# A transformer layer on one core: the turn of the attention output from TensorE to VectorE, two variances from VectorE to ScalarE, and a new order of the work

## The chip, the core and the metric

The kernel runs on one core of one Trainium2 chip. The time is that of the device in microseconds, from one launch of the program. The core has four engines that compute, each with its own queue of instructions in a fixed order: TensorE (PE in the profile, its weight loads PEld), VectorE (DVE), ScalarE (ACT) and GpSimd (POOL). A fifth, SyncE (SP), issues transfers. An instruction that needs another engine's result waits on a semaphore, and all that stands behind it in its queue waits as well.

## What is computed

The input `x` holds 16 sequences of 256 tokens with 256 features. Three residual blocks follow one another, each behind a layer norm:

```python
x = x + attn(layernorm(x))        # a second layer norm with weights inside, 16 heads of 16,
                                  # rotary angles, t = 1 + s + s*s/2 in place of exp, t / sum(t)
x = x + cross(layernorm(x), ctx)  # dec[token] + enc[key] + bias: a sum of two projections to one number
x = x + moe(layernorm(x))         # shared expert + 2 of 16 experts of width 128 for each token
```

In the attention the weighted sum of values `wv` is divided by the sum of the weights of its head and then multiplied by `w_o`. The square in the weights is completed: a = (1 + s/4)^2, and the output adds the sum of the values to each, so that the numerator and (from a column of ones, number 16 of 32) the denominator of every head come out of the same product. All is fp32.

## The kernel before

**Stages.** The first stage is a software pipeline over the 16 sequences. The class `Sequence` has a method for each step, and the list `ORDER` names steps with a lag: (3, "output") in pass i works on sequence i-3. The loop runs over passes i = 0 to 21 (the largest lag is 6) and over the 65 entries of `ORDER` in each; steps whose sequence does not exist are skipped. The schedule is manual: every engine gets its instructions in exactly this order. The list `DRAIN` puts the pieces of the shared expert (`gate_up`, `hidden`, `down`, `add`, for six of eight groups of 512 tokens) between the entries of the last passes, at (pass minus 16, entry). The second stage runs the routed experts by blocks of 128 tokens (`block_tp`, `block_gu`, `block_th`, `block_eo`), which read rows that the first stage wrote to the buffer `listed` in memory (`enlist`), and at the end adds the results. The blocks can begin when the last sequence has been given its places (`place`) and its rows are enlisted.

**A sequence's way**, with lines of the profile. `stat` (L377, L378: two batch-norm operations for each of two token tiles), `scale` (POOL, L384, L385), `norm` (POOL, L393: `h`), `turn_h` (four PE transposes), `copy_h` (ACT, L543), `project` and `project_v` (PE, L553, L601), `sum_values`, `rope` (VectorE, L563 and L569, both read PSUM), `rope_sum` (POOL, L575: `qkr`), `turn_q` and `turn_k` (PE), `copy_q` (L585), `copy_k` (ACT). Then for four groups of four heads `score` (PE, L649), two `square` (ACT, L659) and `product` (PE, L669).

**The steps that the change replaces.** `copy_x` (ACT, L680) brings a pair of groups from PSUM to `xs`, with 32 rows for each head: 16 values, the denominator in row 16, the rest unused. `turn_x` turns a token tile of `xs` with four PE transposes into `xt_ps` (L694). `normalise` takes the reciprocal of column 16 of each head and multiplies (VectorE, L705, L706), from PSUM into `wv`. `turn_w` turns `wv` back with four PE transposes (`tp_w`), and `copy_w` copies it (ACT, L716) to `wvT`, which `output` (PE, L722) multiplies with `wo`. `add_y` (L728) adds to `x`; `decode` computes the statistics of `x` and a weighted sum (L736), `scale_dec` (POOL) scales it, `add_cross` (L748) adds it with `enc_row` and computes the statistics of the third norm; `norm3` (POOL) writes `h3`.

**Routing.** `logits` and `sigmoid` give 16 scores a token; `choose` (VectorE, L792 to L825) finds the two best and marks them in two tiles `hot`; `count` (PE, L784) counts how many tokens ahead chose each expert; `place` (L841 to L881) turns that into row numbers `slots`; `enlist` (POOL, L888) writes rows of `h3` to them, two transfers for each of the two choices.

**Buffers.** PSUM has three one-bank buffers of tag "t", taken in turn by `tp_q`, `tp_k`, `ps_vsum`, `xt_ps`, `pv`, `tp_w`, `ahead`, `pq`, `py`, `tp_h`, `pl`; a step that takes one waits until the third step before it has been read out. Scores have two buffers of two banks, the products one bank.

Of the kernel before, what the change touches and what calls it, by code (L numbers as in the profile page):

```python
# [44 lines left out]
F32 = mybir.dt.float32  # L45
I32 = mybir.dt.int32
AF = mybir.ActivationFunctionType
# [4 lines left out]
P = 128  # L52
# [23 lines left out]
def decoder_kernel(  # L76
# [69 lines left out]

    wo_sb = const.tile([P, KT, D], F32, name="wo_sb")
    for k in range(KT):
        half = w_o[ts(k, P)].rearrange("(j two d) f -> two j d f", two=2, d=HD)
        for i in range(2):  # L150
            nc.sync.dma_start(out=wo_sb[ts(i, P // 2), k], in_=half[i])
# [24 lines left out]
    ones = const.tile([P, P], F32, name="ones")  # L176
# [187 lines left out]
    with tc.tile_pool(name="work", bufs=2) as work, tc.tile_pool(  # L364
# [16 lines left out]
        def rsqrt_eps(var):  # L381

            r = small.tile([P, TT], F32, tag="rs", name="rs")
            nc.gpsimd.tensor_scalar(r, var, 1.0, EPS, ALU.mult, ALU.add)  # L384
            nc.gpsimd.tensor_tensor(r, r, neg_half, ALU.pow)  # L385
            return r

        def normed(h, src, mv, r):

            neg = small.tile([P, TT], F32, tag="neg", name="neg")  # L390
            nc.gpsimd.tensor_scalar(neg, mv[:, :, 0], -1.0, 1.0, ALU.mult, ALU.mult)
            for t in range(TT):
                nc.gpsimd.tensor_scalar(  # L393
                    h[:, t, 0:D], src[:, t], neg[:, t : t + 1], r[:, t : t + 1], ALU.add, ALU.mult
                )
# [72 lines left out]
        class Sequence:  # L468
# [36 lines left out]
            def norm(self):  # L505
                self.h = work.tile([P, TT, D], F32, tag="h", name="h")
                normed(self.h, self.x, self.mv, self.r2)
# [181 lines left out]
            def turn_x(self, q):  # L689
                if q == 0:  # L690
                    self.xt = []
                xt = p_t.tile([P, HEADS, VW], F32, tag="t", name="xt_ps")
                for g in range(GRP):
                    nc.tensor.transpose(  # L694
                        xt[:, ts(g, 4)].rearrange("p h d -> p (h d)"),
                        self.xs[:, g, ts(q, P)], ident,
                    )
                self.xt.append(xt)

            def normalise(self, q):  # L700
                if q == 0:
                    self.wv = work.tile([P, TT, HEADS, HD], F32, tag="wv", name="wv", bufs=1)
                xt = self.xt[q]
                rec = small.tile([P, HEADS], F32, tag="rec", name="rec")
                nc.vector.reciprocal(rec, xt[:, :, HD])  # L705
                nc.vector.tensor_tensor(  # L706
                    self.wv[:, q], xt[:, :, 0:HD],
                    rec.unsqueeze(2).to_broadcast([P, HEADS, HD]), ALU.mult,
                )

            def turn_w(self):
                self.tp_w = self.turned(self.wv.rearrange("p t h d -> p t (h d)"), "tp_w")

            def copy_w(self):
                self.wvT = work.tile([P, KT, T], F32, tag="hT", name="wvT")
                nc.scalar.copy(self.wvT, self.tp_w)  # L716
# [10 lines left out]
            def add_y(self):  # L727
                nc.vector.tensor_tensor(self.x, self.py, self.x, ALU.add)  # L728

            def decode(self):  # L730

                mv = self.mv1 = stats(self.x)
                self.dec = small.tile([P, TT], F32, tag="dec", name="dec")
                for t in range(TT):
                    junk = work.tile([P, D], F32, tag="junk", name="junk_d", bufs=1)
                    nc.vector.scalar_tensor_tensor(  # L736
                        junk, self.x[:, t], mv[:, t, 0:1], mlp_bc[:, D : 2 * D],
                        ALU.subtract, ALU.mult, accum_out=self.dec[:, t : t + 1],
                    )

            def scale_dec(self):
                r = rsqrt_eps(self.mv1[:, :, 1])
# [3 lines left out]
            def add_cross(self):  # L746
                for t in range(TT):
                    nc.vector.scalar_tensor_tensor(  # L748
                        self.x[:, t], self.x[:, t], self.dec[:, t : t + 1], self.enc_row,
                        ALU.add, ALU.add,  # L750
                    )
                self.mv3 = stats(self.x)

            def norm3(self):
                self.h3 = work.tile([P, TT, ROW], F32, tag="h3", name="h3", bufs=3)
                normed(self.h3, self.x, self.mv3, rsqrt_eps(self.mv3[:, :, 1]))
# [23 lines left out]
            def count(self):  # L780

                self.ahead = p_t.tile([P, 2, TT, E], F32, tag="t", name="ahead")
                for i, lhsT in enumerate((tri, ones)):
# [5 lines left out]
            def choose(self):  # L789
# [7 lines left out]
                self.hots = []  # L797
                for i in range(2):
                    hot = tiny_p.tile([P, TT, E], F32, tag=f"hot_{i}", name="hot")
# [13 lines left out]
                    self.hots.append(hot)  # L813
                self.both = tiny_p.tile([P, TT, E], F32, tag="both", name="both")
                nc.vector.tensor_tensor(self.both, self.hots[0], self.hots[1], ALU.add)
# [14 lines left out]
            def place(self):  # L830
# [42 lines left out]
                for i, hot in enumerate(self.hots):  # L873
                    nc.vector.tensor_tensor(hot, hot, rows, ALU.mult)
                    with nc.allow_low_precision(reason="whole numbers below 2**24"):
                        nc.vector.tensor_reduce(self.slots[:, i], hot, AX.X, ALU.add)
# [61 lines left out]
        gate_sb = work.tile([P, D], F32, tag="wv", name="gate_sb", bufs=1)[:E]  # L938
        nc.sync.dma_start(out=gate_sb, in_=gate_w)

        def turn_gate():
# [8 lines left out]
            (2, "rope_sum", 1), (5, "logits"), (1, "copy_h"), (3, "copy_x", 0), (3, "score", 3),  # L950
            (6, "enlist", 0), (1, "project", 0), (2, "turn_q"), (5, "sigmoid"),
            (3, "square", 3, 1), (2, "turn_k"), (0, "load"), (3, "product", 2), (4, "decode"),
            (3, "square", 3, 0), (0, "experts", 0), (2, "copy_q"), (0, "stat"), (1, "encode"),
            (2, "copy_k", 0), (4, "scale_dec"), (3, "product", 3), (2, "copy_k", 1),
            (1, "rope", 0), (3, "copy_x", 1), (1, "sum_values"), (0, "scale"), (2, "score", 0),
            (1, "copy_vsum"), (3, "turn_x", 0), (2, "square", 0, 0), (3, "turn_x", 1),
            (5, "choose"), (6, "enlist", 1), (2, "square", 0, 1), (1, "project_v"),
            (3, "normalise", 0), (0, "norm"), (3, "normalise", 1), (2, "score", 1), (3, "turn_w"),
            (5, "count"), (4, "add_cross"), (5, "place"), (1, "copy_v"), (1, "project", 1),
            (2, "square", 1, 0), (2, "product", 0), (0, "experts", 1), (2, "square", 1, 1),  # L960
            (1, "rope_sum", 0), (3, "copy_w"), (2, "score", 2), (4, "norm3"), (3, "output"),
            (1, "rope", 1), (1, "turn_vsum"), (4, "turn_h3"), (3, "get_enc"), (2, "square", 2, 0),
            (0, "turn_h"), (2, "square", 2, 1), (2, "product", 1), (3, "add_y"), (4, "copy_h3"),
# [4 lines left out]
            (2, 54, 0, "gate_up"), (2, 61, 0, "hidden"), (3, 4, 5, "gate_up"),  # L968
            (3, 14, 1, "gate_up"), (3, 37, 5, "hidden"), (3, 51, 5, "down", 0),
            (3, 51, 1, "hidden"), (3, 54, 4, "gate_up"), (3, 57, 5, "add", 0),  # L970
            (4, 3, 0, "down", 0), (4, 4, 2, "gate_up"), (4, 25, 4, "hidden"), (4, 35, 0, "add", 0),
            (4, 42, 4, "down", 0), (4, 49, 0, "down", 1), (4, 57, 3, "gate_up"),
            (4, 57, 5, "down", 1), (5, 7, 2, "hidden"), (5, 11, 0, "add", 1), (5, 19, 4, "add", 0),
# [267 lines left out]
```

## Time and profile before

| | |
|---|---|
| median of 3 runs | 517.9 us (517.79 to 518.06) |
| the profiled execution | 515.8 us, its span from first to last instruction 514.0 us |
| TensorE clock granted | 0.997 |
| busy PE / PEld / DVE / ACT / POOL | 487.7 / 340.8 / 391.0 / 305.7 / 305.2 us |
| first `qT` copy (L585), then in passes 6 and 7 | 23.73, 96.43, 116.13 us |
| end of the last `place` / first `block_gu` | 363.04 / 375.73 us |

All times inside the run are from the start of the span. A row such as "L636 DVE STREAM_TRANSPOSE vsum<-vsum_rows 128x128 ... x16 | 4.8, 302 | 0.0" is a group of instructions: line, engine, operation, written<-read, shape, number; then busy us in all and mean ns of one; then the engine's idle time ahead of them and what ended it. A row in order of time has its start and length in us first, and in brackets the idle time before it. Rows of one engine may overlap a little, because the next instruction starts while the last drains; so costs on a full engine are taken from start to start.

### The profile page before, as it was taken

What the parts mean: (1) busy time and instruction counts of PE and PEld (TensorE: products, weight loads), DVE (VectorE), ACT (ScalarE), POOL (GpSimd) and SP (SyncE); (2) the same over time, 40 slices, a digit from 0 to 9 for tenths busy, and PEclk for the clock granted to TensorE, in tenths of its full rate; (3) what the DMA queues carried; (4) which work ended last, traced back from release to release, by engine and by line L of the source; (5) the groups of instructions that cost most, each with busy time, mean ns of one, the idle gap of its engine ahead of it and who ended that gap; (6) DMA issues with size and microseconds to landing.
All of it is one profiled execution on the core that took longest, in us unless ns stands there. A gap on an engine that the chain in (4) does not pass through costs nothing. (4 is left out here: it accounts for less than half of the span.)

```text
span 514.0 us, 13014 instructions
## 1 busy us (share of the span) xinstructions
PE 487.7 (95%) x4270; PEld 340.8 (66%) x4270; DVE 391.0 (76%) x1703; ACT 305.7 (59%) x639; POOL 305.2 (59%) x491
## 2 busy tenths in 40 slices
PE   2899999999999999999999999898889999999995
PEld 1456666666766666666666666554578888888883
DVE  5723659988988888988988898899865557777767
ACT  2376776776866767767667767511245555555540
POOL 5743554777768668668668636554326666556560
PEclk9999999999999999999999999999999999999998
DMA  5877255234234233233111011111275457768865
GB/s 177 276 247 223 86 167 164 67 115 135 65 105 134 66 114 116 85 104 104 44 53 55 28 29 54 49 47 43 77 204 171 137 166 268 257 244 281 263 201 201
DMA packets 61138, 69.68 MB, mean 136 GB/s; under 512 B 7164, under 2 KB 52493, under 8 KB 61072
## 3 DMA queue, kind: packets, MB, share of 16 engines
q1 hardware_dynamic: 53760, 50.88, 32.0%
q0 software_dynamic: 6624, 17.05, 9.1%
q10 hardware_dynamic: 688, 0.92, 0.5%
q8 instruction: 35, 0.57, 0.5%
q14 instruction: 31, 0.25, 0.2%
HBM read 36.89 MB, written 33.24 MB: 136 GB/s over the span
## 5 line engine op out<-in xcount | busy, mean ns | idle before, releaser
L659 ACT ACTIVATE a<-sc 128x1024 f32<-128x1024 f32 x128 | 124.1, 1022 | 54.3 <-PE sc L649 54.3
L342 POOL DMA_INDIRECT given<-block_got,block_dest x74 | 72.3, 977 | 61.1 <-ACT block_rowsT L290 41.7
L888 POOL DMA_INDIRECT listed<-h,slots x64 | 66.7, 1043 | 28.8 <-issue 24.1
L649 PE MATMUL sc<-qT,kT 32*128 32x256 f32 x1024 | 74.7, 400 | 0.5 <-ACT a L659 0.2
L312 PE MATMUL block_gu<-wgu_sb,block_rowsT 128*128 x288 | 74.3, 381 | 0.0
L575 POOL TENSOR_TENSOR qkr<-rot,m 128x512 f32<-128x512 f32 x32 | 40.6, 1270 | 47.6 <-DVE m L569 47.6
L669 PE MATMUL av<-a,vaug 128*32 128x256 f32 x1024 | 65.6, 384 | 1.2 <-ACT a L659 1.1
L553 PE MATMUL pq<-wqkv,hT 128*128 128x512 f32 x128 | 64.7, 629 | 1.5 <-ACT hT L543 1.5
L649 PEld LDWEIGHTS sc<-qT,kT 32*128 32x128 f32 x1024 | 47.1, 184 | 17.9 <-issue 11.1
L312 PEld LDWEIGHTS block_gu<-wgu_sb,block_rowsT 128*128 128x128 f32 x288 | 49.2, 190 | 4.2 <-ACT block_hid L318 0.2
L331 DVE COPY block_hidT<-block_th 128x128 f32<-128x128 f32 x74 | 21.6, 292 | 39.1 <-PE block_th L329 38.9
L385 POOL TENSOR_TENSOR rs<-rs,neg_half 128x2 f32<-128x2 f32 x64 | 47.6, 744 | 5.3
L669 PEld LDWEIGHTS av<-a,vaug 128*32 128x32 f32 x1024 | 28.1, 109 | 32.5 <-issue 16.6
L335 PE MATMUL block_eo<-wd_sb,block_hidT 128*128 x148 | 44.0, 380 | 0.0
L377 DVE BATCH_NORM_STATS2 st<-x_all 128x6 f32<-128x256 f32 x96 | 39.3, 409 | 3.2 <-DMA x_all<-in_x_dram 2.7
L318 ACT ACTIVATE block_hid<-block_gu 128x128 f32<-128x128 f32 x74 | 20.5, 278 | 35.1 <-PE block_gu L312 32.5
L341 ACT COPY block_got<-block_eo 128x256 f32<-128x256 f32 x74 | 27.6, 373 | 19.2 <-PE block_eo L335 19.1
L393 POOL TENSOR_SCALAR h<-x_all,neg,rs 128x256 f32<-128x256 f32 x64 | 36.6, 575 | 3.3
L553 PEld LDWEIGHTS pq<-wqkv,hT 128*128 128x128 f32 x128 | 22.3, 194 | 23.0 <-issue 15.4
L563 DVE TENSOR_TENSOR rot<-pq,cosf 128x512 f32<-128x512 f32 x32 | 22.0, 687 | 20.1 <-PE pq L553 18.9
L384 POOL TENSOR_SCALAR rs<-mv 128x2 f32<-128x2 f32 x48 | 10.5, 219 | 40.7 <-DVE mv L378 26.1
L680 ACT ACTIVATE xs<-av,vsum 128x256 f32<-128x256 f32 x64 | 27.0, 478 | 9.6 <-PE av L669 9.6
(187 smaller groups left out, 991.9 us busy)
## 6 DMA issues: line engine op xcount, KB each, us to landing
listed<-empty SPq DMA_DIRECT2D x9, 1056.0 KB
block_rows<-listed SPq DMA_DIRECT2D x68, 132.0 KB
sum<-given SPq DMA_DIRECT2D x15, 512.0 KB
x_all<-in_x_dram SPq DMA_DIRECT2D x16, 256.0 KB
c<-in_ctx_dram SPq DMA_DIRECT2D x16, 256.0 KB
out_dram<-x_all SPq DMA_DIRECT2D x15, 256.0 KB
enc_row<-enc_rows SPq DMA_DIRECT2D x16, 128.0 KB
wgu_sb<-in_L_ffn_w_gate_dram SPq DMA_DIRECT2D x16, 128.0 KB
```

Source lines behind the costliest of these rows:

```text
L312: nc.tensor.matmul(gu, lhsT=self.rowsT[:, k], rhs=wgu_sb[:, ds(e, 1), k].rearrange("p a i m -> p (a i m)"), start=(k == 0), stop=(k == KT ...
L335: nc.tensor.matmul(eo, lhsT=self.hidT, rhs=wd_sb[:, ds(self.e, 1)].rearrange("m a d -> m (a d)"), start=True, stop=True,)
L342: ins = nc.gpsimd.indirect_dma_start(out=given, out_offset=bass.IndirectOffsetOnAxis(ap=self.dest, axis=0), in_=got, in_offset=None, bound ...
L377: nc.vector.bn_stats(st, src[:, t])
L385: nc.gpsimd.tensor_tensor(r, r, neg_half, ALU.pow)
L393: nc.gpsimd.tensor_scalar(h[:, t, 0:D], src[:, t], neg[:, t : t + 1], r[:, t : t + 1], ALU.add, ALU.mult)
L553: nc.tensor.matmul(pq.rearrange("p h i two -> p (h i two)"), lhsT=self.hT[:, k, ts(t, P)], rhs=wqkv[:, k, 0 : 2 * D], start=(k == 0), stop ...
L575: nc.gpsimd.tensor_tensor(self.qkr[:, t], self.rot[t].rearrange("p h d -> p (h d)"), self.m2[t].rearrange("p h i two -> p (h i two)"), ALU ...
L649: nc.tensor.matmul(scs[j // 2][:, j % 2, kt], lhsT=self.kT[rows, g % 2, g // 2, ts(kt, P)], rhs=self.qT[rows, g // 2], start=True, stop=True,)
L659: nc.scalar.activation(a, self.scs[g][i], AF.Square, bias=1.0, scale=HD**-0.5)
L669: nc.tensor.matmul(self.av[ts(j, 32), g % 2], lhsT=self.va[:, kt, head], rhs=self.a[g, j // 2][:, j % 2, kt], start=(kt == 0), stop=(kt == ...
L888: ins = nc.gpsimd.indirect_dma_start(out=listed, out_offset=bass.IndirectOffsetOnAxis(ap=self.slots[:, i, t : t + 1], axis=0), in_=self.h3 ...
```

## The change

1. `turn_x`, `turn_w` and `copy_w` are gone. `normalise(half)` works on a pair of groups in SBUF: VectorE transposes `xs` in 32x32 blocks (a token's head then lies in a row of 32), takes the reciprocal, multiplies, and transposes back in blocks straight into `wvT`. In the new layout the rows of `wvT` are in the order of `w_o`, which is loaded in one transfer in place of four.
2. `add_y` and `add_cross` also give the sum over the features of each token. A new step `spread1` or `spread3` on ScalarE takes the mean from it and sums the squares of x minus mean; the batch-norm operations of these two norms are gone. The first norm keeps them.
3. In `place` the two tiles `hot` are one, and their rows are computed in one product and one reduction.
4. `ORDER` is new and has 63 entries; the largest lag is 7, so there is one pass more. `output` and `add_y` go from lag 3 to 4, `add_cross`, `norm3`, `turn_h3` from 4 to 5, `choose`, `count`, `place` from 5 to 6. `logits` and `sigmoid` stay at lag 5 but stand at the end of the pass. `DRAIN` is new.
5. The tile of ones has 16 columns (its first is broadcast in `count`), and `gate_sb` shares the buffer of `xs`.

```diff
+            def normalise(self, half):
+                if half == 0:
+                    self.wvT = work.tile([P, KT, T], F32, tag="hT", name="wvT")
+                n = T // 32
+                xt = work.tile([P, 2, n, 32], F32, tag="xt", name="xt", bufs=1)
+                nc.vector.transpose(
+                    xt.rearrange("p i n f -> p (i n f)"),
+                    self.xs[:, ts(half, 2)].rearrange("p i t -> p (i t)"),
+                )
+                rec = small.tile([P, 2, n], F32, tag="rec", name="rec", bufs=1)
+                nc.vector.reciprocal(rec, xt[:, :, :, HD])
                 nc.vector.tensor_tensor(
+                    xt[:, :, :, 0:HD], xt[:, :, :, 0:HD],
+                    rec.unsqueeze(3).to_broadcast([P, 2, n, HD]), ALU.mult,
+                )
+                nc.vector.transpose(
+                    self.wvT[:, half].rearrange("p (n i f) -> p n i f", i=2, f=HD),
+                    xt[:, :, :, 0:HD].rearrange("p i n f -> p n i f"),
+                )
...
             def add_y(self):
-                nc.vector.tensor_tensor(self.x, self.py, self.x, ALU.add)
+                self.sum1 = small.tile([P, TT], F32, tag="sum1", name="sum1", bufs=2)
+                for t in range(TT):
+                    nc.vector.scalar_tensor_tensor(
+                        self.x[:, t], self.py[:, t], 0.0, self.x[:, t], ALU.add, ALU.add,
+                        accum_out=self.sum1[:, t : t + 1],
+                    )
+
+            def spread(self, name, total, room):
+                neg = small.tile([P, TT], F32, tag=f"neg{name}", name=f"neg{name}", bufs=2)
+                var = small.tile([P, TT], F32, tag=f"var{name}", name=f"var{name}", bufs=2)
+                nc.scalar.activation(neg, total, AF.Copy, scale=-1.0 / D)
+                for t in range(TT):
+                    nc.scalar.activation(
+                        room[:, t, 0:D], self.x[:, t], AF.Square, bias=neg[:, t : t + 1], scale=1.0,
+                        accum_out=var[:, t : t + 1],
+                    )
+                return neg, var
+
+            def spread1(self):
+                self.neg1, self.var1 = self.spread("1", self.sum1, self.wvT)
...
-                for i, hot in enumerate(self.hots):
-                    nc.vector.tensor_tensor(hot, hot, rows, ALU.mult)
-                    with nc.allow_low_precision(reason="whole numbers below 2**24"):
-                        nc.vector.tensor_reduce(self.slots[:, i], hot, AX.X, ALU.add)
+                nc.vector.tensor_tensor(
+                    self.hots, self.hots, rows.unsqueeze(1).to_broadcast([P, 2, TT, E]), ALU.mult
+                )
+                with nc.allow_low_precision(reason="whole numbers below 2**24"):
+                    nc.vector.tensor_reduce(self.slots, self.hots, AX.X, ALU.add)
...
         ORDER = [
+            (0, "load"), (0, "stat"), (5, "add_cross"), (3, "product", 1), (3, "square", 2, 0),
+            (2, "turn_q"), (2, "turn_k"), (2, "copy_q"), (3, "copy_x", 0), (1, "encode"),
+            (4, "output"), (2, "copy_k", 0), (0, "scale"), (6, "choose"), (3, "score", 3),
+            (0, "experts", 0), (2, "copy_k", 1), (3, "square", 3, 0), (4, "add_y"),
+            (3, "square", 3, 1), (0, "norm"), (1, "project", 0), (3, "product", 2), (1, "rope", 0),
+            (6, "count"), (5, "spread3"), (5, "norm3"), (2, "score", 0), (4, "spread1"),
+            (2, "square", 0, 1), (1, "project", 1), (3, "product", 3), (6, "place"),
+            (2, "square", 0, 0), (1, "rope", 1), (3, "copy_x", 1), (1, "sum_values"),
+            (4, "get_enc"), (2, "score", 1), (4, "decode"), (3, "normalise", 0), (1, "project_v"),
+            (7, "enlist", 1), (1, "rope_sum", 0), (1, "copy_vsum"), (2, "square", 1, 1),
+            (0, "experts", 1), (2, "square", 1, 0), (4, "scale_dec"), (0, "turn_h"),
+            (5, "turn_h3"), (3, "normalise", 1), (1, "rope_sum", 1), (1, "copy_v"),
+            (1, "turn_vsum"), (0, "copy_h"), (6, "enlist", 0), (5, "copy_h3"), (2, "product", 0),
+            (2, "score", 2), (2, "square", 2, 1), (5, "logits"), (5, "sigmoid"),
         ]
         DRAIN = [
+            (2, 32, 4, "gate_up"), (2, 56, 4, "hidden"), (2, 61, 5, "gate_up"),
+            (3, 4, 5, "hidden"), (3, 18, 2, "gate_up"), (3, 25, 3, "gate_up"),
+            (3, 40, 4, "down", 0), (3, 40, 3, "hidden"), (3, 50, 4, "add", 0),
+            (3, 57, 4, "down", 1), (4, 13, 4, "add", 1), (4, 16, 3, "down", 0),
+            (4, 23, 3, "add", 0), (4, 39, 2, "hidden"), (4, 56, 5, "down", 0),
+            (5, 19, 5, "add", 0), (5, 21, 1, "gate_up"), (5, 33, 1, "hidden"),
...
```

The order before had, among the entries around these: (3, "turn_x", 0), (3, "turn_x", 1), (3, "normalise", 0), (3, "normalise", 1), (3, "turn_w"), (4, "add_cross"), (5, "place"), (2, "product", 1) near the end, (3, "copy_w"), (3, "output"), (3, "get_enc") and (3, "add_y") last but one.

## The prediction

> **What bounds the kernel now.** I read the page's busy shares and slices first, then the busy time by 20 us windows, then one period in order of time.
>
> ```profile
> PE 487.7 (95%) x4270; PEld 340.8 (66%) x4270; DVE 391.0 (76%) x1703; ACT 305.7 (59%) x639; POOL 305.2 (59%) x491
> ...
> PE   2899999999999999999999999898889999999995
> ...
> DVE  5723659988988888988988898899865557777767
> ```
> ```profile
> 180.00:200.00 20.00, 20.00 (x219) 13.44 (x218) 17.36 (x75) 14.41 (x26) 14.50 (x26) 1.00 0.32 101
> ...
> 320.00:340.00 20.00, 17.25 (x162) 10.75 (x160) 17.38 (x82) 8.30 (x15) 11.30 (x17) 1.00 0.13 47
> ```
> In 180:200 (columns PE, PEld, DVE, ACT, POOL, then clock) PE is never idle, at the full clock, and VectorE is close behind at 17.36. In 320:340 PE has holes and VectorE has not: the tail belongs to VectorE. A third stage, the expert blocks, begins with the first `block_gu` at 375.73 and is PE back to back; the change does not touch it. So what counts is when the last sequence's `place` ends, 363.04 in the timeline.
>
> One period, PE in order of time, then VectorE's groups of operations:
>
> ```profile
> 178.75 1.09 PE L694 MATMUL xt_ps<-ident,xs 128*128 128x128 f32 x8
> 179.68 1.89 PE L601 MATMUL pv<-wqkv,hT 128*128 128x256 f32 x8
> 181.50 1.15 PE L649 MATMUL sc<-qT,kT 32*128 32x256 f32 x16
> 182.58 0.66 PE L533 MATMUL tp_w<-ident,wv 128*128 128x128 f32 x4
> 183.07 0.31 PE L784 MATMUL ahead<-both,tri 128*128 128x32 f32 x2
> ```
> ```profile
> L377 DVE BATCH_NORM_STATS2 st<-x_all 128x6 f32<-128x256 f32 x96 | 39.3, 409 | 3.2 <-DMA x_all<-in_x_dram 2.7
> ...
> L378 DVE BATCH_NORM_AGGREGATE mv<-st 128x2 f32<-128x6 f32 x96 | 17.5, 182 | 3.3
> ...
> L636 DVE STREAM_TRANSPOSE vsum<-vsum_rows 128x128 f32<-128x128 f32 x16 | 4.8, 302 | 0.0
> ...
> L792 DVE STREAM_TRANSPOSE s<-sT 128x64 f32<-128x64 f32 x16 | 3.8, 236 | 0.0
> ```
> The copy `qT` starts at 175.25 and 194.96: the period is 19.71. Start to start, the eight `xt_ps` transposes hold PE for 179.68-178.75 = 0.93 and the four `tp_w` for 0.49.
>
> **PE.** Both go: 1.42 a sequence, so PE's floor falls to 18.29.
>
> **VectorE**, by start-to-start times of the same period. Now: normalise 1.29, add_cross 0.79 and its statistics 1.10, place 4.16, both ropes 2.40, vsum 0.34, add_y 0.73, statistics 1.08, decode 0.91, stat 1.09, encode 1.11, choose 3.40: 18.40, with 1.2 idle.
> - Out: two statistics, -2.18; normalise, -1.29.
> - In, for each of two halves: a 128x512 block transpose, a reciprocal, a product, a 128x256 transpose. No row has these transposes. 64 more columns cost 302-236 = 66 ns, so 512 columns cost 302+6x66 = 0.70 and 256 cost 0.43. Four and two times the 302 row (1.21, 0.60) are the upper ends; the flatter step from the 32-column row (211 to 236) gives 0.60 and 0.40, the lower. I take the slope of the nearest rows. Reciprocal 0.26 and product 0.42 as L705 and L706 have them. With 0.03 between dependent operations: 1.93 a half, 3.86 in all.
> - add_y becomes two additions with sums; decode's pair of the same form takes 0.91, so +0.20. Sums in add_cross: two accumulator reads of 83 ns, 0.12 after overlap.
> - Both choices at once: four operations of 0.19 (0.65 start to start) become two of about 0.22: -0.2.
>
> Sum 18.40-2.18-1.29+3.86+0.20+0.12-0.20 = 18.9. Some of it is not work but blocking: L868, L869, L870, both L810 and L825 have means 0.58 above their neighbours of the same shape. Free of blocking VectorE needs about 18.4, PE 18.3: VectorE becomes the bound, and the blocking decides the period T.
>
> The blocking, in order of time, VectorE then POOL:
>
> ```profile
> 295.49 1.99 DVE L810 TENSOR_TENSOR hot<-hot,h 128x32 f32<-128x32 f32 x1
> ```
> ```profile
> 295.16 0.97 POOL L888 DMA_INDIRECT listed<-h,slots  x1 [0.30 <-DVE hot L805]
> 296.14 1.28 POOL L575 TENSOR_TENSOR qkr<-rot,m 128x512 f32<-128x512 f32 x1
> ```
> A 0.19 us operation with two SBUF inputs lasted until POOL's addition was over (297.42). [...]
>
> In the new order POOL's `h` stands beside choose, the third norm beside rope and place, one `qkr` addition beside the end of place, the other beside the second normalise. The two products move from PSUM to SBUF and can be blocked now. I take 0.7 a period; the ends are 0.1 (all beside rope, transposes and statistics, which show no such lengthening) and 2.0 (both additions met almost in full, 2x1.28, less what VectorE does meanwhile). T = 19.1, from 18.5 to 20.4.
>
> **ScalarE and POOL.** Each variance adds a copy of 0.2 and two squares with sums; L543 has 0.54 for a square-sized operation with sum, so 1.3 twice, less `copy_w` 0.59: +2.0 on 14.1, 16.1 of 19.1. The square waits for add_y; queued behind it are the squares of score group 0, which PE's next product needs only some 3 us later. POOL loses one 0.2 operation. Without this slack each 0.1 would go on T.
>
> **Walk through the new order** with these durations: `project 1` needs add_y's PSUM buffer, `turn_h` rope's, `output` the second normalise of the pass before. All are met if PE runs up to 1.2 ahead of VectorE, so I count no further wait in the period. `get_enc` is issued 28 tasks (some 8 us) ahead of its reader, before 49 tasks; L748 shows no idle time.
>
> **Fill.** Startup to the first `qT` copy (23.73) stays. From there to the fifth copy (96.43) PE worked 72.7 us. Of that 3x1.42 = 4.3 goes, and one output 1.83, one score 1.08, one `tp_h3` 0.5, logits 0.34 and count 0.35 (4.1) move behind the mark, as these steps come a pass later: 64.3, so VectorE's first full pass starts near 87.
>
> **Steady and tail.** Passes 6 to 15 take 10T, pass 16 T-1.1. Then VectorE alone: passes 17 and 18 (add_cross, choose, add_y, place, decode, normalise) 13.5 each, 19 without normalise 9.65, 20 without add_y and decode 7.8, 21 choose and place 6.9; blocking 1.0; four `hidden` (1.4) and four `add` (0.65) of the shared expert ahead of the last place, 8.2; waits 2.4, as before (0.98+0.38+1.00). The last place ends at 87+11T-1.1+51.4+1.0+8.2+2.4 = 148.9+11T. The same addition on the kernel before, from 309.9, gives 364.0 against 363.04.
>
> T = 19.1 gives 359.0: 4.0 earlier. The gains (fill 8, period 11x0.6) are mostly returned by the seventh pass of the pipeline. Behind the last place four enlists (1.28 each) and the first block loads follow as now, 12.7 to `block_gu`; PE's rest in that time (one gate_up 3.6, eight downs of 0.92: 11.0) fits under it. If it did not, the excess would be added. One load of `wo` for four, the smaller `ones` and `gate_sb` in another buffer cost nothing: their readers come tens of us after the loads, and the gate is turned (34.8) before the first `xs` is written.
>
> Span 514.0-4.0 = 510.0, profiled execution 515.8-4.0 = 511.8. The median of the runs lies 2.1 above the profiled time, so 513.9.
>
> **Rivals.**
> 1. Slower: one `qkr` addition meets decode or a product of normalise in full, each pass. Then T = 18.4+0.58+1.0 = 20.0, the last place 368.9, the time 523.8. It decides from T = 19.5, blocking of 1.1. For it: L810 above, and more two-input SBUF work than before. Against: in 180:200 POOL is free a quarter of the time, and blocked orders shift until they meet less. 0.25.
> 2. VectorE slips past POOL, PE is the bound: T = 18.5, last place 352.4, time 507.3. For it: sums of 18.4 and 18.3. 0.20.
> 3. The transposes cost in proportion to size: +2x(0.51+0.17) = 1.36, T = 20.5, +11.4, time 529. The slope of three rows speaks against it. 0.07.
> 4. The longer tail waits 3 to 5 more, since two gate_ups stand ahead of PE's short steps: no change, 518. 0.08.
> The forecast has 0.40.
>
> **Numbers.** Faster 0.40+0.20 = 0.60, same 0.08, slower 0.32; 0.2% is 1 us, about what can be told apart. 506 takes in rival 2, 525 rival 1; rival 3 is left out.
>
> **What would show it.** Right: `qT` copies 18.5 to 19.5 apart, 128x512 transposes near 0.70, VectorE without idle time from pass 6, last place near 359. Wrong: PE idle behind VectorE by over 1 us a period, products of 1 us or more, VectorE idle in the tail by over 5 us, or `block_gu` over 14 us behind the last place.

## The result: 2.9% slower, and where the time went

The changed kernel takes 533.29 us in the median (529.06 to 534.44, four runs) beside 517.85 for the kernel before on the same chip: a ratio of 1.0286, with an interval of 1.0229 to 1.0343. The forecast was 513.9 in a range of 506 to 525. The profiled execution took 533.32, its span is 531.5, 17.5 more than before.

The page after: busy time of the engines, and the rows of TensorE, VectorE and the granted clock in 40 slices of 13.3 us.

```profile
PE 481.8 (91%) x4078; PEld 319.2 (60%) x4078; DVE 417.8 (79%) x1687; ACT 332.9 (63%) x783; POOL 300.6 (57%) x475
...
PE   2899999999899899989998998986889999999994
...
DVE  5736559899999999999999998898745557777766
...
PEclk9999999999999999999999998998979999999999
```

The two engines have changed places: VectorE now stands at 9 from the ninth slice to the twenty-fourth, and TensorE has holes there. The same windows as before, and the one in which the blocks begin:

```profile
180.00:200.00 20.00, 18.17 (x204) 11.22 (x192) 18.66 (x68) 14.96 (x34) 13.56 (x24) 1.00 0.29 88
320.00:340.00 20.00, 18.53 (x180) 9.75 (x173) 16.77 (x82) 14.54 (x34) 10.75 (x17) 0.91 0.10 34
380.00:400.00 20.00, 15.72 (x67) 11.59 (x66) 9.06 (x40) 6.37 (x18) 3.53 (x4) 0.83 0.56 164
```

In 180:200 TensorE is busy for 18.17 of 20, and it waits for VectorE twice a period (here the bracket names the engine that ended the wait):

```profile
185.02 1.06 PE L529 MATMUL tp_h<-ident,h 128*128 128x128 f32 x8 [1.11 <-DVE m L565]
196.98 0.38 PE L796 MATMUL ahead<-both,tri 128*128 128x32 f32 x2 [0.72 <-DVE norm L828]
```

The copies of `qT` start at 127.60 and, eight periods later, at 294.64: the period is 20.88 in place of 19.71. The 17.5 us divide as follows. The last `place` ends at 375.92 in place of 363.04, +12.9. From there to the first `block_gu` (390.01) it is 14.1 in place of 12.7, +1.4. From there to the end 141.5 in place of 138.3, +3.2. The pipeline is the main part, and in it the period; the fill did become shorter (fifth `qT` copy at 89.25, before at 96.43).

Two operations of VectorE carry the period. VectorE first, then GpSimd, in order of time:

```profile
186.75 1.31 DVE L698 TENSOR_TENSOR xt<-xt,rec 128x256 f32<-128x256 f32 x1
...
189.75 0.42 DVE L698 TENSOR_TENSOR xt<-xt,rec 128x256 f32<-128x256 f32 x1
...
200.91 1.83 DVE L876 SCALAR_TENSOR_TENSOR jump<-firsts,ends 128x16 f32<-128x16 f32 x1
```
```profile
186.51 1.27 POOL L571 TENSOR_TENSOR qkr<-rot,m 128x512 f32<-128x512 f32 x1
...
200.44 0.97 POOL L900 DMA_INDIRECT listed<-h,slots  x1 [0.30 <-DVE ends_new L866]
201.43 1.28 POOL L571 TENSOR_TENSOR qkr<-rot,m 128x512 f32<-128x512 f32 x1
```

An operation of `place` on 16 columns, 0.18 long in the tail, takes 1.83 and is over when GpSimd's first `qkr` addition is over (202.71). The first half's product takes 1.31 and the second half's 0.42: the first ends 0.28 behind the end of the second addition (187.78). From here on, *lengthening* is the sum, over VectorE's operations in one period, of what each takes above the shortest operation of its line and shape in the run, counted from 0.06 up. In the period 169.34 to 190.22 it is 2.94: 1.67 in `place`, 0.88 in the product, 0.39 in three small ones. Without it the period would be 17.9.

### The profile page after: what moved, and what is told of

Its sections match the earlier page's. It is cut to its first block, busy times and chain, and to the rows that moved or that the text cites. A ratio compares the mean times of both kernels' runs of the same rounds, so it can differ in the third digit from the quotient of the medians.

```text
span 531.5 us, 12752 instructions
## 1 busy us (share of the span) xinstructions
PE 481.8 (91%) x4078; PEld 319.2 (60%) x4078; DVE 417.8 (79%) x1687; ACT 332.9 (63%) x783; POOL 300.6 (57%) x475
## 5 line engine op out<-in xcount | busy, mean ns | idle before, releaser
L655 ACT ACTIVATE a<-sc 128x1024 f32<-128x1024 f32 x128 | 125.4, 1020 | 36.6 <-PE sc L645 35.7
L665 PE MATMUL av<-a,vaug 128*32 128x256 f32 x1024 | 69.7, 388 | 0.0
L549 PE MATMUL pq<-wqkv,hT 128*128 128x512 f32 x128 | 66.0, 641 | 0.7 <-ACT hT L539 0.7
L645 PEld LDWEIGHTS sc<-qT,kT 32*128 32x128 f32 x1024 | 47.2, 185 | 19.8 <-issue 6.6
L337 ACT COPY block_got<-block_eo 128x256 f32<-128x256 f32 x74 | 27.6, 373 | 19.2 <-PE block_eo L331 19.1
L529 PE MATMUL tp_h<-ident,h 128*128 128x128 f32 x128 | 19.5, 290 | 20.2 <-DVE m L565 10.7
L387 POOL TENSOR_SCALAR h<-x_all,neg,rs 128x256 f32<-128x256 f32 x64 | 35.5, 560 | 3.3
L711 PE MATMUL py<-wo_sb,wvT 128*128 128x256 f32 x128 | 32.0, 390 | 0.8 <-ACT sT L790 0.5
L597 PE MATMUL pv<-wqkv,hT 128*128 128x256 f32 x128 | 31.9, 392 | 0.3 <-ACT vsum_rows L627 0.3
```

The costliest lines, as they stand in the source:

```text
L387: nc.gpsimd.tensor_scalar(h[:, t, 0:D], src[:, t], neg[:, t : t + 1], r[:, t : t + 1], ALU.add, ALU.mult)
L549: nc.tensor.matmul(pq.rearrange("p h i two -> p (h i two)"), lhsT=self.hT[:, k, ts(t, P)], rhs=wqkv[:, k, 0 : 2 * D], start=(k == 0), stop ...
L645: nc.tensor.matmul(scs[j // 2][:, j % 2, kt], lhsT=self.kT[rows, g % 2, g // 2, ts(kt, P)], rhs=self.qT[rows, g // 2], start=True, stop=True,)
L655: nc.scalar.activation(a, self.scs[g][i], AF.Square, bias=1.0, scale=HD**-0.5)
L665: nc.tensor.matmul(self.av[ts(j, 32), g % 2], lhsT=self.va[:, kt, head], rhs=self.a[g, j // 2][:, j % 2, kt], start=(kt == 0), stop=(kt == ...
L711: nc.tensor.matmul(self.py[:, q], lhsT=self.wvT[:, k, ts(q, P)], rhs=wo_sb[:, k], start=(k == 0), stop=(k == KT - 1),)
```

## The experiments

Theory A: GpSimd's two `qkr` additions hold VectorE off its operations with two SBUF inputs, and that is the loss. Rival B: VectorE's own added work is the loss. Rival C: the new order with its seventh pass. Rival D: TensorE's clock at the end. Ratios are to the kernel before, run on the same chip each time; periods and lengthenings are the mean over eight periods, from the seventh copy of `qT` to the fifteenth.

| kernel | ratio (interval) | period | lengthening a period | last place |
|---|---|---|---|---|
| before | 1 | 19.71 | 0.55 | 363.04 |
| changed | 1.0286 (1.0229 to 1.0343) | 20.88 | 2.92 | 375.92 |
| e1_short_sum | 0.9874 (0.9837 to 0.9912) | 18.97 | 0.65 | 356.43 |
| e2_turns_first | 0.9995 (0.9966 to 1.0024) | 19.33 | 1.95 | 364.23 |
| e3_rope_pair | 1.0279 (1.0214 to 1.0344) | 20.01 | 2.02 | 376.62 |
| e4_both | 1.0264 (1.0226 to 1.0303) | 20.00 | 1.29 | 375.93 |
| d1_double | 1.0490 (1.0431 to 1.0550) | 22.01 | 3.67 | 389.86 |
| e5_covered | 0.9984 (0.9946 to 1.0021) | 19.40 | 0.74 | 364.32 |
| e6_covered_busy_pe | 0.9964 (0.9938 to 0.9989) | 19.36 | 0.74 | 364.16 |
| e8_av_joined | 0.9984 (0.9957 to 1.0010) | 19.36 | 2.12 | 364.36 |
| e9_covered_short | 0.9917 (0.9889 to 0.9944) | 19.44 | 0.82 | 360.96 |
| w1_busy_pe | 1.0226 (1.0183 to 1.0270) | 20.89 | 2.87 | 376.28 |
| p1_turns_only | 1.0620 (1.0602 to 1.0638) | 22.25 | 0.95 | 397.29 |
| p2_spread_only | 1.0051 (1.0030 to 1.0072) | 19.71 | 0.47 | 364.74 |
| p23_spread_hots | 1.0053 (1.0037 to 1.0070) | 19.71 | 0.21 | 364.56 |
| p123_old_order | 1.0562 (1.0545 to 1.0580) | 21.46 | 1.36 | 390.35 |

**e1_short_sum: the additions made short.**

```diff
-   self.qkr[:, t], self.rot[t] (all 512 columns), self.m2[t], ALU.add
+   self.qkr[:, t, 0:HD], self.rot[t][:, 0], self.m2[t][:, 0], ALU.add      # qkr zeroed once
```

> Leaves out part of the rotation: GpSimd's two qkr additions work on 16 of 512 columns each, the other columns of qkr stay zero. Everything else as in the changed kernel. Theory A (the two additions hold VectorE off its operations with two SBUF inputs, 2.5 to 2.9 us a period): L876 falls from 1.83 to about 0.2 us, the first half's product on L698 from 1.31 to 0.42, the period from 20.88 to 18.1-18.6 (PE at 18.3 is then as near the bound as VectorE), and with 11 periods the time to 503-510 us. Rival B (VectorE's own added work, block transposes and sums, is what costs): the period stays above 20.3 and the time above 526. Rival C (the seventh pass and the tail cost more than thought): the period falls to 18.1-18.6, but the time stays above 515.

VectorE, with the lines of this kernel (L878 is the operation of `place`, L700 the product), then GpSimd:

```profile
190.43 0.18 DVE L878 SCALAR_TENSOR_TENSOR jump<-firsts,ends 128x16 f32<-128x16 f32 x1
195.48 0.42 DVE L700 TENSOR_TENSOR xt<-xt,rec 128x256 f32<-128x256 f32 x1
197.60 0.42 DVE L700 TENSOR_TENSOR xt<-xt,rec 128x256 f32<-128x256 f32 x1
```
```profile
192.91 0.25 POOL L573 TENSOR_TENSOR qkr<-rot,m 128x16 f32<-128x16 f32 x1
```

Both long waits are gone, with VectorE's instructions the same as in the changed kernel, and a loss of 2.9% turns into a gain of 1.3%. So A holds against B. But the period is 18.97 (19.04 in the first six) and not 18.1 to 18.6, with TensorE busy without a gap in 180:220, and the time, 515.7, is above A's 503 to 510: 11 periods of 0.5 explain most of that, and this chip was 0.6% slower (520.98 for the kernel before; the ratio on 517.85 gives 511.3). What holds the period at 19 is asked again below. (With other values in `qkr` the tokens choose other experts, so the end of this kernel is not to be compared closely.)

**e2_turns_first: both transposes and reciprocals ahead of both products.** The second half's turned tile goes into the half of `xs` that has been read.

```diff
-  half 0: transpose, reciprocal, product, transpose   ...   half 1: the same
+  transpose 0, reciprocal 0, transpose 1, reciprocal 1, product 0, transpose, product 1, transpose
```

> Normalise as one task: both 128x512 block transposes and both reciprocals first, then the two products and back transposes; nothing left out, the additions stay where they are. Theory A: the second addition (186.51 to 187.78 in the changed kernel) then lies beside transposes and reciprocals, the product on L698's line is 0.42 twice, the period falls by 0.9 to about 20.0 and the time by 10 to about 523; the wait in place (L876, 1.83) stays. Rival B: no change, period 20.9, 533. A rival within A: the addition meets something else instead (decode of the same period), and the gain is under 0.3 a period.

```profile
197.09 0.98 DVE L756 SCALAR_TENSOR_TENSOR junk_d<-x_all,neg,mlp_bc 128x256 f32<-128x256 f32 x1
...
200.30 1.09 DVE L709 TENSOR_TENSOR xt<-xt,rec 128x256 f32<-128x256 f32 x1
```
```profile
196.48 1.30 POOL L571 TENSOR_TENSOR qkr<-rot,m 128x512 f32<-128x512 f32 x1
...
199.82 1.28 POOL L571 TENSOR_TENSOR qkr<-rot,m 128x512 f32<-128x512 f32 x1
```

The gain is larger than expected and from another place. The first addition slid out of `place` to lie mostly beside the second rope (195.89 to 197.1), and what it still reaches is decode, by 0.5. The second still meets the first product, by 0.67. The lengthening fell by 0.97, the period by 1.55 (the other 0.6 is not accounted for here): the loss moves with the position of the additions, which B cannot explain. The run holds a small check of its own: in one of the eight periods the first addition lay beside `place` again (an operation at 215.16 lasts 1.97), and that period took 20.12, the seven others 19.1 to 19.3. This kernel and the kernel before cannot be told apart.

**e3_rope_pair and e4_both: the second rope straight behind the first, e4 with e2's edit as well.**

```diff
-  (1, "project", 0), (3, "product", 2), (1, "rope", 0), ... (1, "project", 1) ... (6, "place") ... (1, "rope", 1)
+  (1, "project", 0), (1, "project", 1), (3, "product", 2), (1, "rope", 0), (1, "rope", 1), ... (6, "place")
-  (7, "enlist", 1), (1, "rope_sum", 0)
+  (5, "norm3"), (1, "rope_sum", 0), ... (7, "enlist", 1)
```

> Order alone: project 1 straight behind project 0 and rope 1 straight behind rope 0, ahead of place; the first addition stands ahead of enlist 1 in GpSimd's queue, so it runs beside rope 1, which reads PSUM. The second addition stays behind scale_dec. Nothing left out. Theory A: L876 falls to 0.2-0.7 (two DMA_INDIRECT still run beside place), the period to 19.2-19.9, the time to 515-522; L698 stays near 0.8 in the mean. Rival B: no change, 533. Rival E (PE's new order makes project 1 wait for PSUM or ScalarE): L876 is short, yet the period does not fall, and PE and VectorE show idle time.

> The two edits together (rope 1 behind rope 0 with the first addition beside it, and both transposes of normalise ahead of its products); nothing left out. Theory A: both long waits go, VectorE needs 18.0-18.6 a period and PE 18.3, the period is 18.3-18.9 and the time 505-512, faster than both kernels. Rival B: 533. If the two waits are not independent (GpSimd shifts when the first one goes and its second addition meets another operation with two SBUF inputs), the period is 19.3-20 and the time 516-524.

Neither came in time. The period is 20.0 in both, 0.9 less than in the changed kernel, but the last `place` ends where it did there (376.62 and 375.93 beside 375.92), chiefly because the fill is longer: the sixth copy of `qT` starts at 114.28 in e3 and at 111.71 in e4, in the changed kernel at 107.28. The first addition did not lie beside the second rope: in e4 GpSimd's `norm3`, ahead of it, waited 3.28 for ScalarE's sums of the third norm, and the addition started at 199.80, beside `place` again (an operation there lasts 1.03 in place of 0.18). And with both projections in front (3.63 of TensorE in one piece) VectorE waits up to 0.5 at each rope of e4, the later scores wait for ScalarE's squares, and in e4, with only 1.29 of lengthening, TensorE is busy for 19.8 of 20. That is near rival E of the expectation: in e3 the period fell by what the lengthening fell, in e4 by half of it, and the rest went into the new order's waits and the fill.

**d1_double: each addition issued twice.**

```diff
+  for again in range(2):
       nc.gpsimd.tensor_tensor(self.qkr[:, t], self.rot[t], self.m2[t], ALU.add)
```

> Changed kernel with each of GpSimd's two qkr additions issued twice (the same values again). GpSimd has over 6 us of 20 to spare, so by its own work nothing is to be expected. Theory A: L876 in place lasts up to 1.28 longer (3.1), the second addition's double meets the first product and, behind it, the second half's product or stays beside transposes; VectorE's period grows from 20.88 to 22-23 and the time by 12-23 to 545-556. Rival B (VectorE's own work is the cost): period 20.9, time 533.

```profile
210.32 1.88 DVE L881 TENSOR_TENSOR past<-past,jump 128x32 f32<-128x32 f32 x1
...
212.34 1.20 DVE L883 TENSOR_TENSOR rows<-rows,past 128x32 f32<-128x32 f32 x1
```
```profile
210.86 2.63 POOL L572 TENSOR_TENSOR qkr<-rot,m 128x512 f32<-128x512 f32 x2
```

The ratio grew from 1.0286 to 1.0490 by work of an engine that is idle a third of the time. Against the expectation no operation was held through both additions, but one by each: between the two VectorE slipped one operation in. The periods come as 24.9, 18.4 and 21.4 by turns; two whole rounds of these give 21.56 in the mean, the eight of the table 22.01. So 2.6 us more of additions cost 0.7 to 1.1 of period.

**e5_covered: additions placed where VectorE reads PSUM or has one SBUF input.** From the lesson of e2: both additions one behind the other, from the second rope on; VectorE behind that rope does the two transposes with their reciprocals, then decode, then the products.

```diff
-  (4, "decode"), (3, "normalise", 0), (1, "project_v"), (7, "enlist", 1), (1, "rope_sum", 0), ...
-  (3, "normalise", 1), (1, "rope_sum", 1)
+  (3, "normalise", 0), (4, "decode"), (1, "project_v"), (7, "enlist", 1), (1, "rope_sum", 0), (1, "rope_sum", 1), ...
+  (3, "normalise", 1)                    # 0: both turns and reciprocals, 1: both products
```

> Changed kernel with both qkr additions put behind enlist 1 (one behind the other), and on VectorE behind rope 1: both 128x512 block transposes with their reciprocals, then decode, then the products. Nothing left out. By the run with the transposes first (period 19.3, of it 1.89 blocking: decode 0.51, product 0.67, small ones 0.71), Theory A: decode and both products unblocked (0.47, 0.42), only the small 0.7 left (third norm and DMA_INDIRECT beside choose and place). VectorE then needs 18.1-18.4 and PE's chain through rope 1 sets the period: 18.7-19.0. Last place 356-361, time ratio to the kernel before 0.985-0.995. Rival: the additions wait for rope 1 or the transposes end sooner than they, and decode or a product is met again: period 19.2-19.6, ratio 0.998-1.006.

The blocking by the additions is gone: in one period they run from 196.44 to 198.95, beside a rope operation of 0.68, transposes of 0.70 and 0.65 and reciprocals of 0.25, and the products behind them take 0.42 and 0.38 (0.74 is left, most of it beside `h`, as in e1). The period is no shorter than e2's: it falls in the range of the rival, but not for the rival's reason. Instead VectorE now waits for TensorE at the first rope:

```profile
190.32 0.69 DVE L559 TENSOR_TENSOR rot<-pq,cosf 128x512 f32<-128x512 f32 x1 [0.49 <-PE pq L549]
```

**e8_av_joined and e9_covered_short: what sets 19.4?** Both stand on the covered order with w1's edit (below). e8 puts `product` 3 beside `product` 2; e9 shortens the additions as e1 does.

```diff
e8  -  (1, "project", 1), (3, "product", 3), (6, "place")
    +  (3, "product", 2), (3, "product", 3), (1, "rope", 0)
e9  +  rope_sum as in e1_short_sum
```

> The covered order with the repeated down products, and product 3 moved up beside product 2, as the kernel before had them (there one av block of 32 took 1.75; apart they take 1.00 and 0.89). If PE's chain sets the period of 19.35: it falls by 0.1-0.3 to about 19.1-19.2 and the ratio to the kernel before from 0.996 to 0.988-0.994. If VectorE sets it: no change, 19.35 and 0.996. Rival: product 3 waits for ScalarE's square there and PE loses what it gained.

> The covered order with the repeated down products, and the two additions cut to 16 of 512 columns each (leaves out part of the rotation; the other columns of qkr stay zero). If the additions still blocked in the covered order, the period falls from 19.35 to 18.6-18.8. If PE's chain sets it, the period stays at 19.1-19.4 although GpSimd has 2.5 us less to do, and the blocking that is left on VectorE is the 0.7 of the third norm and DMA_INDIRECT.

e9: with 2.1 us less for GpSimd to do the period is 19.44, alternating between 19.1 and 20.0, so the additions have nothing more to do with it; VectorE waits up to 1.0 for `pq`. What is left is TensorE's chain, with its waits for VectorE and ScalarE; that it holds the period near 19 is read from these waits and no edit shows it. e8 does not help: joined, the two products took 1.86, apart 1.00+0.89, so TensorE saved next to nothing, and the shift moved an addition back onto `place` (an operation of 1.88), and VectorE filled the period again.

**w1_busy_pe and e6_covered_busy_pe: TensorE kept busy ahead of the blocks.**

```diff
+  again = {(1, 1): 3, (0, 1): 2}.get((self.n, half), 1)
-  for i in range(2):
+  for i in [0, 1] * again:
       nc.tensor.matmul(self.eo[half][:, i], ...)
```

> Changed kernel with two of the shared expert's last down products issued three times and twice over (same values written again), so that TensorE stays busy between the last place and the first blocks. Rival D (part of the loss is TensorE's clock after idle time, granted 0.83 in 380:400, where four shared_eo and the first four block_gu last 2.08 and 2.04 instead of 1.1): these fall to 1.1, last place to first block_gu falls from 14.1 to about 13 and the time by 1.5-2.5, period unchanged at 20.88. Without the clock's part: the repeats cost their own 3 us or nothing, the short forms stay at 2.0.

> The covered order and the repeated down products together. Theory A with D: 1.5-2.5 us below the covered order alone, ratio 0.98-0.99; without D's part equal to it or 1-3 us above.

The changed kernel, and then w1, at the first blocks:

```profile
386.40 2.08 PE L941 MATMUL shared_eo<-wd_sb,shared 128*128 128x256 f32 x4
390.01 2.04 PE L308 MATMUL block_gu<-wgu_sb,h3T 128*128 x4 [1.53 <-issue]
```
```profile
387.23 1.13 PE L942 MATMUL shared_eo<-wd_sb,shared 128*128 128x256 f32 x4 [0.24 <-ACT h3T L286]
389.89 1.10 PE L308 MATMUL block_gu<-wgu_sb,h3T 128*128 x4 [1.53 <-DVE block_weight L293]
```

The slow clock is gone (1.00 in 380:400 in place of 0.83), and the forms last 1.1 as D says. The time did not follow: the first `block_gu` comes at 13.6 behind the last `place` in place of 14.1, the last one, 121.7 behind the first, in place of 120.4, and the end 155.9 behind the last `place` in place of 155.6. So D is not shown: the clock was low, but other waits of the block stage stand behind it. The two ratios' intervals overlap, and so do e6's and e5's. e6 is the one complete kernel that measures faster than the kernel before, by 0.36%; e1 and e9 leave work out.

**The parts alone, in the old order.** p1 has the turns on VectorE, p2 the variances on ScalarE, p23 also both choices' rows at once, p123 all three. All four use the smaller tile of ones, for room.

```diff
p1    -  turn_x, turn_w, copy_w            +  normalise(half) of the changed kernel at the old places
p2    +  (4, "spread1") behind (1, "copy_h"), (4, "spread3") behind (2, "square", 1, 0)
p23   +  one tile hots
p123  all of these
```

> The kernel before with the first part of the change alone, in the old order: weighted values turned and normalised by VectorE in halves, TensorE's xt_ps and tp_w gone. Statistics and choices as before. By the rows: VectorE 18.4-1.29+3.9 = 21.0 a period and PE 18.3, so VectorE is the bound and any blocking comes on top: period 21-22.5, time 525-540. Theory A (two qkr additions block): at least one operation of 1 us or more on VectorE a period, period 21.5-22.5. Rival B (only the work counts): period 21.0, time about 526.

> The kernel before with the second part alone, in the old order: two variances on ScalarE from sums of the additions (spread1 ahead of decode, spread3 behind add_cross); also the smaller ones, for room. TensorE's turns stay. VectorE falls from 18.4 to about 16.6 a period, PE stays at 19.7: the period stays 19.7-20.0. The tail, where VectorE sets the pace, loses 1.8 a pass in four passes: time 509-514, faster. Rival: ScalarE, in order, waits for add_y or add_cross and holds squares and copies up, the period goes above 20 and the time to 518 or more.

> As the one with the second part alone, with both choices' rows at once added. Another 0.2-0.4 less on VectorE in each pass of the tail, nothing in the period: 1-2 us less than the second part alone, 508-513.

> All three parts of the change in the old order (six passes deep, the steps at their old places, spread1 ahead of decode, spread3 behind add_cross). VectorE about 18.5 clean, PE 18.3. Rival C (the new order with its seventh pass is what costs): period 18.5-19.2 and the time 498-508. Theory A (the additions block wherever two-input operations lie beside them): the period is 19.5-21 here too, and the time 508-522, the seventh pass's tail of some 7 us being saved.

p1 is the loss: 1.062 (549.6, above the 525 to 540 expected), with a period of 22.25 in the mean. Its periods take 21.0 and 23.5 by turns. In the short ones VectorE waits for nothing by more than 0.2 and none of its operations lasts 1 us: here B is right, for VectorE's work itself comes to 21.0, as expected, 1.3 over TensorE's 19.71 before. In the long ones an addition holds the first operation of `add_cross` (0.44 in the short ones), as A says, and at the next rope VectorE waits for TensorE. So B's part of the 2.5 a period is 1.3, and the other half comes with the meeting and the wait behind it. VectorE, GpSimd, and last TensorE, which waits longer than in the changed kernel:

```profile
196.48 1.54 DVE L741 SCALAR_TENSOR_TENSOR x_all<-x_all,dec,enc_row 128x256 f32<-128x256 f32 x1
...
211.45 0.69 DVE L560 TENSOR_TENSOR rot<-pq,cosf 128x512 f32<-128x512 f32 x1 [1.69 <-PE pq L550]
```
```profile
196.47 1.27 POOL L572 TENSOR_TENSOR qkr<-rot,m 128x512 f32<-128x512 f32 x1
```
```profile
204.88 0.63 PE L530 MATMUL tp_h<-ident,h 128*128 128x128 f32 x4 [2.29 <-DVE m L566]
```

p2 came out 0.5% slower where 1 to 2% faster was expected, and p23 the same as p2. The period stayed at 19.71 and VectorE had 1.8 a pass less to do, but the last `place` still ended at 364.74, since its waits in the tail grew from 2.4 to 7.7 us:

```profile
DVE count L864 <- PE ahead L807: 2.2, 3, 1.4
DVE rec L705 <- PE xt_ps L694: 1.8, 2, 1.2
DVE s L815 <- ACT sT L801: 1.3, 2, 1.0
DVE x_all L730 <- PE py L722: 0.9, 1, 0.9
```

(VectorE's waits from 313 to 365, with the engine that ended them, total, number, longest.) Work taken off VectorE there became waiting for other engines' short steps. p123 at 1.056, far from the 498 to 522 us that both theories expected, says that parts 2 and 3 give back little of part 1 in the old places. One reason stands in its rows: `decode` now waits 1.5 to 1.8 in each period for ScalarE's sums, and a product of `normalise` is held by an addition as well (1.15 to 1.45).

```profile
201.66 0.48 DVE L749 SCALAR_TENSOR_TENSOR junk_d<-x_all,neg,mlp_bc 128x256 f32<-128x256 f32 x1 [1.60 <-ACT neg L733]
```

The new order gives back half of the loss. Rival C falls: the new order helps, by the difference of 1.056 and 1.029.

## Why the prediction was wrong

**The blocking: the step that failed.** It was taken at 0.7 a period, from 0.1 to 2.0; it is 2.92, of which 2.55 is the two additions. Two things were mis-sized. The upper end took 2x1.28 as the most that both could cost, less what VectorE does meanwhile; but VectorE is held before the addition's recorded start. The blocked operations began 0.52 (changed kernel), 0.54 (d1) and 0.51 us (e8) ahead of it and stood until it was over, so that an addition of 1.28 took 1.67 in `place`. The row of the kernel before that the prediction showed had this already: L810 began at 295.49, the addition at 296.14. And 0.7 rested on the argument that blocked orders shift until they meet less. In the changed kernel they do not: there GpSimd is tied to VectorE by its own waits (the first addition stands behind `enlist` 1, the second behind `scale_dec`, which waits for decode), so the two meet at the same places in every period (the product in each, at 1.31, and an operation of `place`, at 1.83 or more). In d1 and p1 the meetings do change from period to period, and the mean period is no shorter for it.

An operation of VectorE with two SBUF inputs that lay beside an addition stood until the addition was over: in the changed kernel the product ends 0.28 or 0.29 behind it, each of thirteen times, and the operations of `place` 0.03 to 0.06. One that reads PSUM kept its length: in the kernel before, `add_y` at 189.44 takes 0.69, the mean of all sixteen, beside the addition of 189.17 to 190.45. In `place` the VectorE operation has the earlier recorded start, by 0.52, and waits all the same. Most operations beside an indirect transfer, which is GpSimd's work too, kept their lengths: in e5 two of them (194.04 to 196.43) lay beside ten operations of `place`, and none of the ten was longer. Two operations with one input were: L825 takes 0.34 in place of 0.16 in nine of its sixteen instances before, and L863 takes 0.30 to 0.32 in place of 0.17 in eight of its sixteen in the changed kernel, and each time it ends 0.01 to 0.04 ahead of the transfer's recorded end. Why these two is open.

**VectorE's clean work** was predicted at 18.4 and is 17.9. The transposes cost what the slope of the three rows gave: 709 and 445 ns for 0.70 and 0.43. The additions with sums were cheaper (0.68 for the pair in place of 0.93), the rows of both choices as predicted (0.23, 0.22). Rival 3 is refuted by the first of these.

**TensorE's floor** of 18.29 was too low. Added start to start in e1, without a wait of 0.36 in one score, its period is 18.69. What the change took away is as said, but the new order splits `av` (1.00+0.89+1.00+0.97 in place of 1.75+1.00+0.89) and `ahead` takes 0.56 in place of 0.36. With VectorE at 17.9 and 0.7 of blocking, 18.6, and TensorE at 18.7, each waiting for the other at places, e1, e5 and e9 stand at 19.0 to 19.4; which of these places sets it is open. So rival 2 (period 18.5, 507) was out of reach as well, and the forecast of 19.1 would have needed all of the blocking to vanish.

**Rival 1** named the mechanism, with a chance of 0.25: one addition met in full, 20.0 and 523.8. It was two, one of them in `place` and not in decode or a product.

**Fill, tail, blocks.** The fill gained 7.2 (8 predicted; its own sum, 23.7+64.3, gives 88.0, and the prediction went on with 87). The sum 148.9+11T gives 378.6 for T = 20.88, and 375.9 was measured; for e1's 18.97 it gives 357.6, and 356.4 was measured: the walk through the pipeline held. The 12.7 from the last `place` to the first `block_gu`, taken as unchanged, came out 1.4 longer, and the block stage, taken as untouched, 3.2 longer. The kernels of the old order (p1, p2, p23, p123) need 151 to 153 us from the last `place` to the end, like the kernel before (151.0); those of the new order 154 to 158. Why is not settled. The chain at the end of the changed kernel passes through transfers where before it stayed on TensorE:

```profile
515.93 4.69 DMA given<-block_got,block_dest
520.67 3.72 DMA sum<-given
```

That alone does not explain it: p1 and p2, in the old order, end through the same transfers and need 153. The clock was low at the start of the blocks (0.83 in 380:400), but w1, with 1.00 there, ends no sooner (155.9 behind the last `place` beside 155.6).

Of what was to show the forecast wrong, three came true: products of 1 us or more, TensorE idle behind VectorE by more than 1 us a period (1.83), `block_gu` 14.1 behind the last `place`.

## What to carry to other kernels

Before moving operations from PSUM to SBUF on VectorE, list what GpSimd does at that place in the steady period, and count each addition like these (128x512 from SBUF, 1.28) in full, with half a microsecond ahead of it where an indirect transfer stands in front, against the first operation with two SBUF inputs beside it: here that was 0.88 in the product and 1.67 in `place`. A mean of blocking over the kernel before (0.55) says nothing on the new order (2.92). Such additions are better put beside work that reads PSUM or has one input, which in e5 kept its length (0.68 for a rope operation, 0.70 and 0.65 for the transposes), and whether they lie there has to be looked up in the trace, since a new wait elsewhere (e3) shifts them back. Work can be moved to another engine only until that engine reaches the floor of the one relieved (part 1 alone put VectorE's work 1.3 us a period past the old floor, and the period 2.5), and here two engines near the same floor lost 1.5 to 4% to each other (19.0 to 19.4 beside 18.7).

## What the runs showed of the hardware that was not expected

- A VectorE operation of 16 columns (0.18 us) was held for 1.83 us by one GpSimd addition of 1.28.
- Operations that began 0.50 to 0.65 us before the addition's recorded start were held: 0.65 in the kernel before, 0.50 to 0.64 in ten passes of the changed kernel, 0.54 in d1 and 0.51 in e8; one that ended 0.54 ahead of it (e8, at 195.04) was not. Each time an indirect transfer stands directly ahead of the addition; two such transfers without an addition made none of ten operations longer (e5, 194.04 to 196.43). Why the hold begins so early is open.
- Two additions back to back let one VectorE operation through between them (d1: 210.32 to 212.2, then 0.18, then 212.34 to 213.54).
- An idle time of TensorE of 3.68 us (to 362.31, in the changed kernel's tail) was followed by `ahead` at 0.64 and 0.61 in place of 0.38 and 0.39, at a granted clock of 0.50 (362.3 to 364).
